# Order of stores, row transfers and loads in the first half of a Strassen MLP (DiT block, one core)

## Chip, cores and metric

One core of one Trainium2 chip runs the whole program. The metric is the time of one execution on the device in microseconds; lower is better.

## The reference

A transformer block with adaptive modulation (two sequences of 2048 tokens, 576 features, 16 heads), all in float32. The part that matters here is the MLP that ends it:

```python
xn2 = _ln(x, 1e-06)
xn2 = xn2 * (1 + sc_mlp[:, None, :]) + sh_mlp[:, None, :]
h = jax.nn.gelu(xn2 @ w1 + b1, approximate=False)     # 576 -> 2304
m = h @ w2 + b2                                       # 2304 -> 576
x = x + g_mlp[:, None, :] * m
```

## The kernel before

The kernel does modulation, attention and the output projection for one batch entry after the other, and then the MLP for all 4096 tokens. Both MLP products are computed by a seven-product (Strassen-Winograd) scheme, and the MLP is split into two halves by a round trip through DRAM.

**First half.** The tokens form NB = 8 blocks of 512, and the hidden features form HF = 9 pairs of column groups. A *job* is one block with one group: block n = job // 9, f = job % 9, so there are 72 jobs. A loop takes two jobs at a time, an even one and an odd one. In each job:

- PE runs `whole_part` (14 matmuls over the full 128-row chunks; the product number 1 goes to the bank `one`, written last) and `last_part` (8 matmuls for the last 64 features). Two sets of banks, one for even and one for odd jobs, hold the results.
- `hidden_made` empties the banks: ACT copies product 1 into a buffer `cs`, DVE combines the other six with it (four instructions), ACT applies Gelu (two), POOL makes the four sums that are the operands of the second half. There are three buffers `cs`, used in turn, so the copy of job j overwrites what job j - 3 left.
- `hidden_stored(job)` is a transfer, issued by SP, of one `cs` (896 KB) to the tensor `operands` in DRAM. It has to be done before the copy of three jobs later.

Beside this, `ahead(job)` prepares the rows of the next blocks, four tiles of 128 tokens (i = 0 to 3) per block, in four steps that lie two or three jobs apart: "load" fetches rows (SP), "turn" normalizes them (DVE statistics, an ACT square root, DVE) and writes them turned in 32 x 32 squares to DRAM (four SP transfers), "read" fetches them by feature (three SP transfers), "modulate" applies scale and shift (six ACT instructions and one of POOL). A generator says which step of which tile falls to which job; with a block that begins on an even job, nearly all fall to the even jobs, with the others to the odd ones. When a block begins, `token_sums` (four DVE instructions) makes the sums that its products need; for a block that begins on an odd job they are placed inside the even job before it.

SP, POOL, ACT and DVE run in the order of the program text (PE too), so in each pair of jobs the order on SP is: `ahead(job)`, `hidden_stored(job-2)`, `ahead(job+1)`, `hidden_stored(job-1)`, and then what the weights need. A transfer that waits on SP holds up all behind it.

In the same loop DVE makes the seven combinations of w2, two steps per pair of jobs (`weights_made`, in five chunks c = 0 to 3 and the tail): SP loads pieces into `w_first`, DVE adds and subtracts, SP stores the results with `stored` to the tensor `w_kept` in DRAM, 31 transfers of one 144-column piece for all seven products. At the end SP loads three of the combined weights (products 1, 2 and 6) back into `w_first` (`firsts_loaded`).

**Second half.** 56 products: for each block seven, in the order 1, 2, 6, 5, 7, 4, 3. Each needs one operand (1152 KB, `operand_loaded`), kept in three buffers in turn, and one combined weight (2232 KB, `weights_loaded`, seven in all). `sums_made(i)` makes the sums of an operand, on POOL for even and on DVE for odd products; `multiplied` is PE's part, some 7.8 us; `combined_blocks` and `finished` are DVE's, with the residual rows `xr` that SP loads for four of the seven products.

Where the buffers lie: operand 0 is in its own memory. When the last block's jobs have used a column of the first weight `wb`, its memory is free; there lie operand 1 and the weights of products 5, 7 and 4. Operand 2, the weight of product 3 and the sums of odd products lie in a new pool `hs`, which is opened after the first half. In the loop's last jobs SP loads operand 1 (after jobs 64 and 65, `at_job == 2`), weight 5 (after 66 and 67) and weight 7 (after 68 and 69); at the start of the second half it loads operand 2, then two gate rows, and in the loop of the products operand i + 3 once product i has been multiplied, and weights 4 and 3 after products 1 and 2.

Of the kernel before, what the change touches and what calls it, by code (L numbers as in the profile page):

```python
# [8 lines left out]
F32 = mybir.dt.float32  # L9
# [7 lines left out]
P = 128  # L17
# [5 lines left out]
FULL = 4  # L23
# [8 lines left out]
def dit_block(  # L32
# [724 lines left out]
    def block_of_small():  # L757
# [1275 lines left out]
        def ahead(job):  # L2033


            n, f = divmod(job, HF)

            def at(**offsets):
                for i in range(TPB):
                    for what, offset in offsets.items():  # L2040
                        m, g = divmod(job - 2 * i - offset, HF)
                        if g == 0 and m + 1 < NB and (m, i) > (0, 0):
                            yield what, (m + 1, i)

            for what, todo in at(turn=-2, read=0, modulate=2, load=-5):
                m, i = todo
                block, cols = xnts[m % 2], slice(i * P, (i + 1) * P)
                if what == "load":
                    rows_ahead[todo] = mlp_loaded(*todo, nc.sync)
                elif what == "turn":  # L2050
                    rows_ahead[todo] = tile_turned(rows_ahead[todo], nc.sync)
                elif what == "read":
                    turned_loaded(block, cols, rows_ahead.pop(todo), nc.sync)
                else:
                    turned_modulated(block, cols, 2, m // NBLK)
# [4 lines left out]
        def weights_made(c):  # L2060

            tail = c == 2 * FULL
            depth = 1 if tail else 2
            all_ = w_first[:, 0, 0 : 7 * depth * HALF].rearrange("p (i k f) -> p i k f", i=7, k=depth)
            more = w_first[:, 1, 0 : 28 * QUARTER].rearrange("p (i j f) -> p i j f", i=7, j=4)
            side = w_first[:, 2, 0 : depth * HALF].rearrange("p (k f) -> p k f", k=depth)
            rows = w2.rearrange("(k p) f -> p k f", p=P)
            tt = nc.vector.tensor_tensor

            def load():  # L2070
                for dst, k, n in ((all_[:, 0], 0, 0), (side, 0, 1), (all_[:, 1], 1, 0), (all_[:, 2], 1, 1)):
                    k0 = k * HF + c
                    nc.sync.dma_start(
                        out=dst, in_=rows[:, k0 : k0 + (depth - 1) * FULL + 1 : FULL, n * HALF : (n + 1) * HALF]
                    )

            def stored(j, src):
                nc.sync.dma_start(
                    out=w_kept[:, :, j * QUARTER : (j + 1) * QUARTER].rearrange("i p f -> p i f"), in_=src
                )  # L2080

            left, right = slice(0, QUARTER), slice(QUARTER, HALF)
            y11, y12 = all_[:, :, 0, left], all_[:, :, 0, right]
            steps = [
                load,
                lambda: None,
                lambda: tt(all_[:, 4], side, all_[:, 0], ALU.subtract),
                lambda: tt(all_[:, 6], all_[:, 2], side, ALU.subtract),
                lambda: tt(all_[:, 5], all_[:, 2], all_[:, 4], ALU.subtract),
                lambda: tt(all_[:, 3], all_[:, 5], all_[:, 1], ALU.subtract),  # L2090
            ]
            if tail:
                return [
                    *steps,
                    lambda: (
                        tt(more[:, :, 0], y12, y11, ALU.subtract),
                        [stored(28 + j, src) for j, src in enumerate((y11, y12, more[:, :, 0]))],
                    ),
                    *[lambda: None] * 3,
                ]  # L2100
            y21, y22 = all_[:, :, 1, left], all_[:, :, 1, right]
            return [
                *steps,
                lambda: (
                    tt(more[:, :, 1], y12, y11, ALU.subtract),
                    [stored(FULL * j + c, src) for j, src in enumerate((y11, y21, y22))],
                ),
                lambda: tt(more[:, :, 3], y22, y12, ALU.subtract),
                lambda: tt(more[:, :, 2], y22, more[:, :, 1], ALU.subtract),
                lambda: (  # L2110
                    tt(more[:, :, 0], more[:, :, 2], y21, ALU.subtract),
                    [stored(FULL * (3 + j) + c, more[:, :, j]) for j in range(4)],
                ),
                *[lambda: None] * 3,
            ]
# [4 lines left out]
        def firsts_loaded():  # L2120
# [1 line left out]
                weights_loaded(m, w_first[:, i, :])  # L2122

        spots = wb.rearrange("p f m k c -> p (f m k c)")
        operand.append(spots[:, 0 : HF * PAIR].rearrange("p (f c) -> p f c", f=HF))
        weight_spots = {
            m: spots[:, HF * PAIR + i * WSIZE : HF * PAIR + (i + 1) * WSIZE] for i, m in enumerate((5, 7, 4))
        }
        sums = {0: [first_sums[:, j] for j in range(3)]}

        def operand_parts(i):
# [21 lines left out]

        making_weights = [do for c in (0, 1, 2, 3, 2 * FULL) for do in weights_made(c)] + [firsts_loaded]

        rows_ahead = {}
        for i in (1, 2):
            nc.vector.memset(xs["tiles"][0][0:1, 0:1], 0.0)
            rows_ahead[1, i] = mlp_loaded(1, i, nc.gpsimd)
# [1 line left out]
        with tc.manual_schedule(  # L2161
            engines={mybir.EngineType.SP, mybir.EngineType.Pool, mybir.EngineType.Activation}
        ):
            for job in range(0, NB * HF, 2):
                (n0, f0), (n1, f1) = divmod(job, HF), divmod(job + 1, HF)
                ahead(job)
                hidden_stored(job - 2)
                whole_part(n0, f0, 0)
                if f1 == 0:
                    token_sums(n1)  # L2170
                last_part(n0, f0, 0)
                ahead(job + 1)
                hidden_stored(job - 1)
                hidden_made(n0, f0, 0)
                whole_part(n1, f1, 1)
                last_part(n1, f1, 1)
                if f1 == HF - 1 and n1 + 1 < NB:
                    token_sums(n1 + 1)
                hidden_made(n1, f1, 1)
                for _ in range(2):  # L2180
                    if job >= 2 and making_weights:
                        making_weights.pop(0)()
                if job == 2 * HF:
                    operand_loaded(0)
                if job == 4 * HF:
                    sums_made(0, slice(0, 3))
                at_job = job + 1 - (NB - 1) * HF
                if at_job == 2:
                    operand_loaded(1)
                for i, m in enumerate((5, 7)):  # L2190
                    if at_job == (4, 6)[i]:
                        weights_loaded(m, weight_spots[m])
        for job in (NB * HF - 2, NB * HF - 1):
            hidden_stored(job)
        stack.close()
# [4 lines left out]
        hs, close_hs = opened("hs")  # L2200
        rows_in_order = tc.manual_schedule(engines={mybir.EngineType.SP})
        rows_in_order.__enter__()
        operand.append(hs.tile([P, HF, PAIR], F32, name="operand2"))
        operand_loaded(2)
        weight_spots[3] = hs.tile([P, WSIZE], F32, name="w_last")
        ws = {m: w_first[:, i, :] for i, m in enumerate((1, 2, 6))} | weight_spots
        sums[0].append(hs.tile([P, FULL, P], F32, name="fourth"))
        sums_made(0, slice(3, 4))
        sums_odd = hs.tile([P, 4, FULL, P], F32, name="sums")
        sums[1] = [sums_odd[:, j] for j in range(4)]  # L2210
        ws = {m: w.rearrange("p (j f) -> p j f", f=QUARTER) for m, w in ws.items()}

        def stationaries(i):
# [4 lines left out]
        def multiplied(i):  # L2218
# [6 lines left out]
            for group in ((1,), (2, 6), (5, 7), *last):  # L2225
                ps = bank()[:, 0 : 2 * QUARTER].rearrange("p (a f) -> p a f", a=2)
                outs[group] = ps
                for a, m in enumerate(group):
                    out_m[m] = ps[:, a, :]
                    ends = m == group[-1]  # L2230
                    for c in range(FULL):
                        nc.tensor.matmul(  # L2232
                            out_m[m],
                            stationary[m][:, c, :],
                            w[:, FULL * (m - 1) + c, :],
                            start=a == 0 and c == 0,
                            stop=ends and c == FULL - 1 and m not in tails,
                        )
                    if m in tails:
                        t, j = tails[m]  # L2240
                        nc.tensor.matmul(  # L2241
                            out_m[m], x_[:, 2 * FULL, t * P : (t + 1) * P], w[:, j, :], start=False, stop=ends
                        )
# [59 lines left out]
        for i, (n, m) in enumerate(products):  # L2303
# [9 lines left out]
            xr = residual_rows(n, *quadrant, gate_bias) if quadrant else None  # L2313
            out_m, outs = multiplied(i)
            operand_loaded(i + 3)
            if i in (1, 2):
                weights_loaded((4, 3)[i - 1], weight_spots[(4, 3)[i - 1]])
            if i + 1 == len(products):
                last_finished(z12, out_m, outs, n, *quadrant, xr, gate)
                break  # L2320
# [68 lines left out]
```

## Time and profile before

| | us |
|---|---|
| median of three runs (3114.15 to 3115.0) | 3114.4 |
| the profiled execution, its own time | 3114.03 |
| its span, first to last instruction | 3111.4 |
| PE busy | 3059.0 (98%) |
| DVE busy | 1661.6 (53%) |
| ACT busy | 1491.8 (48%) |
| POOL busy | 954.1 (31%) |

The granted TensorE clock is 0.998 of full speed over the span. In the profile a row of a timeline gives the start (us from the span's first instruction), the duration, the engine, the line of the kernel, what is written from what, and a count of like instructions in a row; in brackets stands how long the engine had been idle before it, and what ended that. "SPq" is SP issuing a transfer. In the table by stretches the columns are the length, the busy time of PE, PE's weight load, DVE, ACT and POOL (with counts), the granted clock, the busy share of the DMA engines and what they moved in GB/s. A line of the chain of waits gives start, duration and what the end was waiting for.

### The profile page before, as it was taken

The page shows a single profiled execution, that of the slowest core. Times are in us where ns is not written, and L with a number is a line of the kernel's source. Part 1 is how long each engine was busy: PE and PEld are TensorE (multiplying, and loading weights), DVE is VectorE, ACT ScalarE, POOL GpSimd, SP SyncE. Part 2 cuts the span into 40 slices and gives each one's busy share as a digit, 9 for nine tenths or more (in the row PEclk, how much of TensorE's full clock was granted, in tenths as well). Part 3 has the DMA queues.
Part 4 walks back from the last instruction along what each step waited for, and adds up shares of the span by engine and source line. Part 5 has one row for each costly group of instructions (what it writes and reads, how often), then busy time and mean ns, then how long its engine had stood idle before and what let it go on. Part 6 is the DMA issues. An engine that isn't in the chain of part 4 may idle for free.

```text
span 3111.4 us, 51193 instructions
## 1 busy us (share of the span) xinstructions
PE 3059.0 (98%) x19079; PEld 1909.4 (61%) x19079; DVE 1661.6 (53%) x2525; ACT 1491.8 (48%) x2909; POOL 954.1 (31%) x1191
## 2 busy tenths in 40 slices
PE   8999999999999999999999999999999899999999
PEld 6884333333333788533333333368888788999999
DVE  6773444444443566444434444446666554676666
ACT  2336666766667023566666666633555543000000
POOL 4650100132231355200011210013444444555554
PEclk9999999999999999999999999999999999999999
DMA  5773332233332554311122322155877778755554
GB/s 150 188 145 86 102 93 58 66 94 98 93 100 68 193 128 79 85 47 34 47 57 73 86 66 59 57 146 168 247 225 224 216 215 295 289 192 194 205 191 158
DMA packets 443832, 413.52 MB, mean 133 GB/s; under 512 B 231512, under 2 KB 375896, under 8 KB 435448
## 3 DMA queue, kind: packets, MB, share of 16 engines
q1 hardware_dynamic: 398176, 310.84, 33.8%
q0 software_dynamic: 35968, 94.02, 11.2%
q10 hardware_dynamic: 9432, 5.31, 0.7%
q8 instruction: 153, 2.51, 0.3%
q14 instruction: 103, 0.84, 0.1%
HBM read 244.81 MB, written 154.75 MB: 128 GB/s over the span
## 4 chain that ended last, share of the span: by engine, by line
PE 85%; DMA 4%; DVE 4%; ACT 3%; SPq 2%; issue 1%; POOL 1%; DVEq 0%; ACTq 0%; POOLq 0%
PE b L1549 29%; PE b L1536 20%; PE b L2232 12%; PE s L1143 6%; PE s L1229 5%; PE m L1983 4%; PE s L411 4%; DMA operands<-cs 3%; PE b L2241 2%; SPq L1047 1%; PE s L1145 1%; PE m L1997 1%; PE s L1235 1%; PE one L1983 1%; ACT xnt L1064 1%
## 5 line engine op out<-in xcount | busy, mean ns | idle before, releaser
L1540 ACT ACTIVATE pt<-b 128x512 f32<-128x512 f32 x2048 | 1057.4, 608 | 481.4 <-PE b L1549 267.6
L1549 PE MATMUL b<-pt,vt 128*64 128x512 f32 x4096 | 935.0, 598 | 1.8 <-ACT pt L1540 1.8
L1549 PEld LDWEIGHTS b<-pt,vt 128*64 128x64 f32 x4096 | 271.8, 136 | 583.9 <-issue 437.7
L1536 PE MATMUL b<-qm,km 32*128 32x512 f32 x4096 | 563.9, 613 | 0.1
L1601 DVE TENSOR_TENSOR ot<-b,ot 128x512 f32<-128x512 f32 x192 | 132.7, 691 | 586.9 <-PE b L1549 586.9
L1536 PE MATMUL b<-qe,ke 16*128 16x512 f32 x2048 | 420.6, 791 | 0.0
L1536 PEld LDWEIGHTS b<-qm,km 32*128 32x128 f32 x4096 | 191.0, 184 | 271.0 <-ACT pt L1540 211.1
L1983 PE MATMUL m<-xnt,wb 128*128 128x256 f32 x864 | 213.2, 383 | 17.9 <-DVE cs L2017 17.0
L1143 PE MATMUL s<-wq,xnt 128*128 128x288 f32 x864 | 226.7, 406 | 2.0 <-ACT xnt L400 2.0
L1568 DVE RECIPROCAL den<-den 128x512 f32<-128x512 f32 x64 | 213.5, 3337 | 11.0 <-DMA den<-den_dram 11.0
L2249 ACT COPY one<-b 128x144 f32<-128x144 f32 x55 | 15.4, 279 | 410.2 <-PE b L2232 395.1
L1983 PE MATMUL m<-s,wb 128*128 128x256 f32 x864 | 210.0, 379 | 0.0
L1599 DVE COPY ot<-b 128x512 f32<-128x512 f32 x64 | 44.3, 691 | 273.0 <-PE b L1549 273.0
L1983 PEld LDWEIGHTS m<-xnt,wb 128*128 128x128 f32 x864 | 159.5, 191 | 41.4 <-DVE cs L2017 20.9
L1143 PEld LDWEIGHTS s<-wq,xnt 128*128 128x128 f32 x864 | 157.8, 190 | 37.5 <-ACT xnt L400 2.7
L1983 PEld LDWEIGHTS m<-s,wb 128*128 128x128 f32 x864 | 164.2, 190 | 22.3
L1536 PEld LDWEIGHTS b<-qe,ke 16*128 16x128 f32 x2048 | 107.1, 184 | 113.6 <-issue 112.8
L2021 ACT ACTIVATE cs<-cs,b_sb 128x512 f32<-128x512 f32 x144 | 100.5, 721 | 131.5 <-DVE cs L2016 131.4
L1064 ACT ACTIVATE xnt<-xnt,mod 128x128 f32<-128x128 f32 x244 | 99.9, 481 | 116.7 <-DMA weight_sums<-sums_kept 50.8
L1658 POOL DMA_DIRECT2D spare<-in_x_dram x32 | 17.8, 555 | 443.0 <-DVE met L796 443.0
L2023 POOL TENSOR_TENSOR cs<-cs 128x256 f32<-128x256 f32 x72 | 59.5, 826 | 294.1 <-ACT cs L2021 294.1
L2010 DVE TENSOR_TENSOR cs<-m,cs 128x512 f32<-128x512 f32 x72 | 48.8, 678 | 158.7 <-ACT cs L2009 111.1
(322 smaller groups left out, 4479.3 us busy)
## 6 DMA issues: line engine op xcount, KB each, us to landing
operands<-cs SPq DMA_DIRECT2D x72, 896.0 KB
operand<-operands SPq DMA_DIRECT2D x37, 1152.0 KB
wb<-operands SPq DMA_DIRECT2D x19, 1152.0 KB
spare<-in_x_dram POOLq DMA_DIRECT2D x64, 288.0 KB, 3.2
x_dram<-spare POOLq DMA_DIRECT2D x64, 288.0 KB, 2.5
qm<-qk SPq DMA_DIRECT2D x256, 64.0 KB
den<-den_dram SPq DMA_DIRECT2D x128, 128.0 KB
w_kept<-w_first SPq DMA_DIRECT2D x31, 504.0 KB
```

What stands on the lines that cost most here:

```text
L411: nc.tensor.matmul(outs[a], stationary(k, a), moving(k, a), start=(first and k == 0), stop=(not first and k == FULL - 1),)
L1064: nc.scalar.activation(part, part, AF.Identity, **affine(which, k, b))
L1143: nc.tensor.matmul(out_a, full[:, k, :], wq[:, k, f], start=k == 0, stop=False)
L1229: nc.tensor.matmul(out[m], x_[:, k, :], w_(k), start=k == 0, stop=k == 1 and m == 6)
L1536: nc.tensor.matmul(ps, k[r, keys], q[r, :], start=first, stop=not first)
L1540: nc.scalar.activation(pt[:, h, :], banks[2 * c + h], AF.Exp, scale=SCALE)
L1549: nc.tensor.matmul(acc[64 * h : 64 * h + 64, :], vt[:, v0 : v0 + 64], pt[:, h, :], start=pt is pts[0][0], stop=pt is pts[-1][0],)
L1568: nc.vector.reciprocal(den, den)
L1601: nc.vector.tensor_tensor(ot, acc, ot, ALU.add)
L1983: nc.tensor.matmul(out_m[m], wb[:, f, slot[m], k, :], moving[m](k), start=k == 0 and m in (1, 2, 5, 6), stop=k == 1 and m == 1,)
L2021: nc.scalar.activation(part, part, AF.Gelu, bias=b1_sb[:, g : g + 1])
L2232: nc.tensor.matmul(out_m[m], stationary[m][:, c, :], w[:, FULL * (m - 1) + c, :], start=a == 0 and c == 0, stop=ends and c == FULL - 1 and ...
```

## The change

1. `ahead` goes through the steps in the order read, turn, load, modulate, and within each over the tiles; before, it went through the tiles, and within each through turn, read, modulate, load. In a job in which a tile is turned and another modulated, the square root now comes first on ACT.
2. `hidden_stored(job - 2)` comes before `ahead(job)`, and `hidden_stored(job - 1)` before `ahead(job + 1)`.
3. The tensor `w_kept` is laid out by chunk, so the pieces of one chunk lie side by side: a full chunk is stored in three transfers (1, 2 and 4 columns wide) instead of seven, the tail in two instead of three. They are put on a list and issued at the start of the next pair of jobs, behind `hidden_stored(job - 2)`. PE's index into the weight follows.
4. Operand 2 lies in the memory of `wb` beside operand 1, and both are loaded after jobs 66 and 67; weight 5 is loaded after jobs 68 and 69. The sums of odd products lie in `wb` too. Weights 4 and 3 lie in `hs`. Weights 7, 4 and 3 are loaded after products 0, 1 and 2.

```diff
-                for i in range(TPB):
-                    for what, offset in offsets.items():
+                for what, offset in offsets.items():
+                    for i in range(TPB):
...
-            for what, todo in at(turn=-2, read=0, modulate=2, load=-5):
+            for what, todo in at(read=0, turn=-2, load=-5, modulate=2):
...
-            def stored(j, src):
-                nc.sync.dma_start(
-                    out=w_kept[:, :, j * QUARTER : (j + 1) * QUARTER].rearrange("i p f -> p i f"), in_=src
-                )
+            def stored(j, count, src):
+                j += 7 * c if not tail else 28
+                dst = w_kept[:, :, j * QUARTER : (j + count) * QUARTER].rearrange("i p f -> p i f")
+                to_store.append(lambda: nc.sync.dma_start(out=dst, in_=src))
...
-                        [stored(28 + j, src) for j, src in enumerate((y11, y12, more[:, :, 0]))],
+                        stored(0, 2, all_[:, :, 0, :]),
+                        stored(2, 1, more[:, :, 0]),
...
-                    [stored(FULL * j + c, src) for j, src in enumerate((y11, y21, y22))],
+                    stored(0, 1, y11),
+                    stored(1, 2, all_[:, :, 1, :]),
...
-                    [stored(FULL * (3 + j) + c, more[:, :, j]) for j in range(4)],
+                    stored(3, 4, more.rearrange("p i j f -> p i (j f)")),
...
-        operand.append(spots[:, 0 : HF * PAIR].rearrange("p (f c) -> p f c", f=HF))
+        OSIZE = HF * PAIR
+        operand += [spots[:, i * OSIZE : (i + 1) * OSIZE].rearrange("p (f c) -> p f c", f=HF) for i in range(2)]
         weight_spots = {
-            m: spots[:, HF * PAIR + i * WSIZE : HF * PAIR + (i + 1) * WSIZE] for i, m in enumerate((5, 7, 4))
+            m: spots[:, 2 * OSIZE + i * WSIZE : 2 * OSIZE + (i + 1) * WSIZE] for i, m in enumerate((5, 7))
         }
+        odd_sums = spots[:, 2 * OSIZE + 2 * WSIZE :][:, 0 : 4 * FULL * P].rearrange(
+            "p (j k c) -> p j k c", j=4, k=FULL
+        )
...
                 (n0, f0), (n1, f1) = divmod(job, HF), divmod(job + 1, HF)
+                hidden_stored(job - 2)
+                while to_store:
+                    to_store.pop(0)()
                 ahead(job)
-                hidden_stored(job - 2)
...
                 last_part(n0, f0, 0)
+                hidden_stored(job - 1)
                 ahead(job + 1)
-                hidden_stored(job - 1)
...
-                if at_job == 2:
+                if at_job == 4:
                     operand_loaded(1)
-                for i, m in enumerate((5, 7)):
-                    if at_job == (4, 6)[i]:
-                        weights_loaded(m, weight_spots[m])
+                    operand_loaded(2)
+                if at_job == 6:
+                    weights_loaded(5, weight_spots[5])
...
-        operand.append(hs.tile([P, HF, PAIR], F32, name="operand2"))
-        operand_loaded(2)
-        weight_spots[3] = hs.tile([P, WSIZE], F32, name="w_last")
+        for m in (4, 3):
+            weight_spots[m] = hs.tile([P, WSIZE], F32, name=f"w{m}")
...
-                            w[:, FULL * (m - 1) + c, :],
+                            w[:, 7 * c + m - 1, :],
...
-            if i in (1, 2):
-                weights_loaded((4, 3)[i - 1], weight_spots[(4, 3)[i - 1]])
+            if i < 3:
+                weights_loaded((7, 4, 3)[i], weight_spots[(7, 4, 3)[i]])
```

5 lines of the change are left out of this document (2 added, 3 removed).

## The prediction

> **What bounds the kernel now.** I read the page's parts 1 and 4 first, then the order of PE in time, then who waited for whom, then SP's queue.
>
> ```profile
> span 3111.4 us, 51193 instructions
> PE 3059.0 (98%) x19079; PEld 1909.4 (61%) x19079; DVE 1661.6 (53%) x2525; ACT 1491.8 (48%) x2909; POOL 954.1 (31%) x1191
> 2122.76:2660.83 538.07, 513.42 (x2593) 454.66 (x2593) 307.45 (x519) 260.68 (x457) 238.87 (x318) 0.99 0.77 233
> ```
>
> The third line is the table by stretches for the first MLP half: 538 us, DMA engines 77% busy. PE is the bound, so a change pays only where PE stands still. PE's timeline gives that:
>
> ```profile
> 2122.76 1.96 PE L1983 MATMUL m<-xnt,wb 128*128 128x256 f32 x8 [0.90 <-issue]
> 2194.69 1.99 PE L1983 MATMUL m<-xnt,wb 128*128 128x256 f32 x8 [1.46 <-DVE cs L2017]
> 2343.57 1.99 PE L1983 MATMUL m<-xnt,wb 128*128 128x256 f32 x8 [0.74 <-DVE cs L2017]
> 2467.78 1.99 PE L1983 MATMUL m<-xnt,wb 128*128 128x256 f32 x8 [1.13 <-DVE cs L2017]
> 2579.12 2.00 PE L1983 MATMUL m<-xnt,wb 128*128 128x256 f32 x8 [0.35 <-DVE cs L2017]
> 2628.22 1.89 PE L1983 MATMUL m<-xnt,wb 128*128 128x256 f32 x8
> 2636.35 2.07 PE L1983 MATMUL one<-xnt,wb 128*128 128x256 f32 x4 [2.78 <-ACT cs L2009]
> 2660.83 2.12 PE L2232 MATMUL b<-w_first,operand 128*128 128x144 f32 x16
> ```
>
> Except for 2636.35 (inside job 68) these are starts of jobs 0, 10, 30, 46, 61, 68 and of the first product, "job 72". An undisturbed job takes 7.00 us (61 to 68: 49.10 / 7), so 72 want 504.0 and got 538.07: 34.07 us are lost. Start minus first start minus 7 x number gives the lag: 1.93 at job 10, 10.81 at 30, 23.02 at 46, 29.36 at 61, 29.46 at 68, 34.07 at the end. So 1.93 is lost before job 10, then 8.88, 12.21 and 6.34 in three clusters, 0.10, and 4.61 in job 68. The clusters lie in blocks 2, 4 and 6 and run into the next one: nine jobs a block, so these blocks begin on an even job, and their row work falls into the even jobs.
>
> ```profile
> ACT cs L2009 <- DMA operands<-cs: 70.3, 17, 11.0
> DVE cs L2010 <- ACT cs L2009: 111.1, 32, 12.2
> PE m L1983 <- DVE cs L2017: 17.0, 18, 1.6
> ```
>
> From the waits (us, times, longest): ACT's copy into a cs buffer waits until the store of three jobs ago has left it, DVE waits for ACT, PE for DVE. Why the store is late shows the timeline of all engines in job 20 (last row: the copy of job 21):
>
> ```profile
> 2266.96 0.73 POOL L2026 TENSOR_TENSOR cs<-cs 128x256 f32<-128x256 f32 x1
> 2270.88 1.64 ACT L1064 ACTIVATE xnt<-xnt,mod 128x128 f32<-128x128 f32 x4
> 2272.32 0.21 DVE L279 BATCH_NORM_AGGREGATE mv<-st 128x2 f32<-128x12 f32 x1
> 2273.31 1.28 ACT L281 ACT_TABLE_LOAD   x1
> 2274.80 0.35 ACT L2009 COPY cs<-one 128x256 f32<-128x256 f32 x1
> 2276.55 1.98 SPq L1047 DMA_DIRECT2D turned<-squares  x4
> 2278.64 1.09 SPq L2031 DMA_DIRECT2D operands<-cs  x2
> 2282.97 0.37 ACT L2009 COPY cs<-one 128x256 f32<-128x256 f32 x1 [1.92 <-DMA operands<-cs]
> ```
>
> POOL finished job 18's sums at 2267.69. SP issued their store at 2278.64, 10.95 us later, having sat in order behind the four row transfers, which waited for DVE. It landed at 2282.9, when PE had long wanted the buffer (job 21 ends near 2279.8).
>
> **The change, part by part.** *Stores ahead of row transfers* (SP). With hidden_stored(job-2) first, job 18's store goes at 2267.7 and lands by 2272 to 2276 (4.3 us as above, or 8.8 behind a burst):
>
> ```profile
> 2218.66 8.81 DMA operands<-cs
> 2266.01 9.75 DMA xnt<-turned
> L2078 SPq DMA_DIRECT2D w_kept<-w_first x31: 359/852/3530, 2194.7 to 2590.3; - x31
> ```
>
> That is 3 to 7 us before job 21 wants it, so the clusters should go: 8.88 + 12.21 + 6.34 = 27.43, less two block starts of 1.4 (block starts, below), 24.6. Not all: I keep 1.6 for bursts of weight stores, an estimate (one stall of the size above). Gain 23.0, between 12 and 24.6. What now stands behind the store's wait for POOL on SP are the row transfers, three reads, four turns and a load per row job. A read lands in 9.75 us (second row, from the chain) and is wanted two jobs, 14 us, later: 4.25 us to spare. That hides it.
>
> *Roots ahead of modulations* (ACT). In the same rows ACT modulated from 2270.88 to the table load at 2273.31 (2.4 us), and then took the root. Turned round, it loads the table (1.28 us) and takes the root when mv is ready at 2272.5; the modulations end near 2275.1, where the copy of job 20 began at 2274.80. So the copy is 0.3 late, up to 1.6 where mv is later, and the squares about 2 us earlier. PE wants the copied bank only a job later: 0, bounds +1 and -2 over the half.
>
> *Weight stores in three pieces.* 31 issues become 14 (4 x 3 + 2): 17 x 0.85 us of SP time, which waits anyway; the bytes stay. They go one pair of jobs later, and their next load comes 1.5 pairs after that. Cost 0; the burst behind the 8.81 above (1.0 us of the second cluster's 8.88) now comes behind the even store.
>
> *Block starts.*
>
> ```profile
> 2184.95 1.08 DVE L1953 TENSOR_TENSOR s<-xnt 128x512 f32<-128x512 f32 x1 [0.87 <-ACT xnt L1064]
> 2190.17 0.29 ACT L281 ACTIVATE std<-mv,eps 128x1 f32<-128x1 f32 x1 [3.18 <-DVE mv L279]
> ```
>
> At odd blocks DVE does the token sums and a row's norm before it empties job 8's banks; PE then waits 1.46 (row 2194.69), and likewise two more times, some 4.5 in all. The diff leaves this order. With copies on time the sums may start some tenths earlier: 0.7 gained in all, an estimate, bounds 0 and 4.5.
>
> *Loads at the end of the half.*
>
> ```profile
> 2607.44 2.51 SPq L2118 DMA_DIRECT2D w_first<-w_kept  x3
> 2609.99 0.68 SPq L2152 DMA_DIRECT2D wb<-operands  x1
> 2613.90 0.37 SPq L2031 DMA_DIRECT2D operands<-cs  x1
> 2635.92 0.37 ACT L2009 COPY cs<-one 128x256 f32<-128x256 f32 x1 [11.03 <-DMA operands<-cs]
> wb<-operands SPq DMA_DIRECT2D x19, 1152.0 KB
> wb<-w_kept SPq DMA_DIRECT2D x3, 2232.0 KB
> 2610.00:2620.00 10.00, 10.00 (x51) 8.91 (x51) 2.62 (x5) 2.65 (x5) 4.77 (x7) 1.00 1.03 411
> ```
>
> Job 64's store stood behind three weights (6.86 MB) and operand 1 (1.18 MB), and job 68 lost 4.61. Operand 1 now comes behind that store: at 411 GB/s it lands 2.9 us sooner, the copy at 2633.0, which is PE's own time for that bank; DVE's emptying still makes job 69 about 1.5 late. Gain 3.1, bounds 0 and 4.6. [...] After that, operands 1 and 2 (2.36 MB) take the place of weight 5 (2.29), weight 5 that of weight 7, one block column of wb sooner: equal bytes, 0.
>
> *Start of the second half.*
>
> ```profile
> 2674.01 8.99 DMA xr<-x_dram
> 2681.71 3.21 PE L2232 MATMUL b<-w_first,first_sums 128*128 128x144 f32 x24 [2.42 <-POOL first_sums L2146]
> 2686.00 4.71 DVE L2146 TENSOR_TENSOR sums<-sums,operand 128x512 f32<-128x512 f32 x1
> 2690.76 3.21 PE L2232 MATMUL b<-wb,sums 128*128 128x144 f32 x24 [0.94 <-DVE sums L2146]
> 2696.50 2.12 PE L2232 MATMUL b<-wb 128*128 128x144 f32 x16
> 2704.34 2.12 PE L2232 MATMUL b<-wb,operand 128*128 128x144 f32 x16
> ```
>
> A product takes 7.84 (last two rows); four took 35.67, so 4.31 were lost, first to operand 2 (POOL's sums), then to xr, behind which DVE makes the sums of product 3. Operand 2 is now there; but weight 7 (5.6 us at 411) is queued ahead of xr. Counting from product 0's start, xr landed at 22.2; without operand 2 (2.9) and with weight 7 it lands near 24 to 25. POOL's bias (1.4), DVE's add and two sums (0.7 to 0.8 each) follow in 3.7 if POOL does not slow them: ready at 28.2, wanted at 23.5 + 2.2 = 25.7 (three products and the first row's 2.12 us). Loss 2.5, gain 1.8, bounds +4.3 and -2.8. From product 4 on nothing changes.
>
> **Sum.** 23.0 + 0 + 0 + 0.7 + 3.1 + 1.8 = 28.6. The profiled execution took 3114.03 (2.6 around its span), 0.4 under the median 3114.4: 3085.4 against it, 3086 as a median. Nothing else can be had: 34.07 + 4.31 = 38.4 is all of PE's loss here, which gives 3076.
>
> **Rivals.**
> *Weight 7 takes over.* DVE's second sum stretches to 4.71 beside POOL, as in the row above, and xr is late: the sums are ready at 31.8 instead of 28.2, product 3 loses 6.1, and PE another 1 in coming up again, a loss of 7.1 for my 2.5, so 3114.4 - 24 = 3090. For it: SP's one queue; against: POOL's next sums wait for operand 4, queued later still. [...]
> *The DMA engines become the bound.* Bursts already fill them (1.03 above). If early stores still land late, half of the 24.6 stays: 12.3 + 0.7 + 3.1 + 1.8 = 17.9, so 3096.5. Against: the 8.81 landing would still be in time.
> *It does not do what it says.* The stores were late from DMA alone: 3113. Against: the 10.95 us on SP.
> *Slower: rows come late.* Reads now stand behind a wait for POOL and weight stores that can take 3.53 us to issue. From 4.25 us of delay on, ACT waits in order at the modulation with the cs copies behind it, 27 times (four a block, seven blocks, one done before). Each microsecond past it costs up to 27; past 5.3 it eats the 28.6. At 5.7 us: 3114.4 - 28.6 + 39 = 3125. Against: no ACT wait for a read appears in the waits of before.
>
> **Numbers.** Forecast 0.62, weight 7 0.13, DMA 0.17: all faster, 0.92. No effect 0.04, rows late 0.04. About 0.2%, 6 us, is what a measurement tells apart. Likeliest 3086, its own range 3079 to 3092; the 8-in-10 range reaches from all of the loss gone, 3076, to past the DMA rival, 3100.
>
> **What would show it.** Right: SP's operand store straight after POOL's last sum, ahead of the four turns; the ACT wait for operands<-cs down from 70 us to under 20; blocks 2, 4, 6 at 7.00 us a job; a first half of 506 to 512 us. Wrong: ACT waiting on xnt<-turned, or DMA at 1.0 while the copies still wait; a loss past 6 us before product 4. The forecast fails if PE's stalls only move to another wait in the same jobs.

## The result, and the profile after

The changed kernel takes 3090.7 us (median of four runs, 3090.14 to 3092.17) against 3114.7 for the kernel before in the same session (its three runs above and one of 3119.28): a ratio of 0.992 with the 95% interval [0.9903, 0.9938]. It is faster by 24.0 us where 28.6 were forecast.

The first two lines of the page of the changed kernel, and then its table by stretches (columns as before) for the first MLP half and for the first eight products of the second:

```profile
span 3089.8 us, 51183 instructions
PE 3055.7 (99%) x19079; PEld 1910.9 (62%) x19079; DVE 1666.5 (54%) x2525; ACT 1492.6 (48%) x2909; POOL 956.3 (31%) x1191
```
```profile
2124.64:2632.32 507.68, 505.25 (x2592) 451.83 (x2593) 310.98 (x519) 261.63 (x457) 241.61 (x318) 1.00 0.80 244
2632.32:2705.64 73.32, 66.59 (x514) 66.16 (x513) 50.99 (x73) 3.50 (x10) 34.80 (x28) 0.95 0.71 270
```

The first half shrank from 538.07 to 507.68 us. Where PE still stands shows its timeline in order; these are the first job, all stops of the first half that a wait explains, and products 0, 3, 4, 7 and 8 (of products 3 and 7 the row after the wait):

```profile
2124.64 1.96 PE L1983 MATMUL m<-xnt,wb 128*128 128x256 f32 x8 [0.90 <-issue]
2195.70 2.00 PE L1983 MATMUL m<-xnt,wb 128*128 128x256 f32 x8 [0.83 <-DVE cs L2017]
2322.45 1.99 PE L1983 MATMUL m<-xnt,wb 128*128 128x256 f32 x8 [0.48 <-DVE cs L2017]
2449.20 1.99 PE L1983 MATMUL m<-xnt,wb 128*128 128x256 f32 x8 [0.49 <-DVE cs L2017]
2611.22 2.00 PE L1983 MATMUL m<-xnt,wb 128*128 128x256 f32 x8 [0.62 <-DVE cs L2017]
2632.32 2.12 PE L2238 MATMUL b<-w_first,operand 128*128 128x144 f32 x16
2660.57 4.88 PE L2238 MATMUL b<-wb 128*128 128x144 f32 x24 [2.36 <-DVE wb L2152]
2667.98 2.12 PE L2238 MATMUL b<-wb 128*128 128x144 f32 x16
2698.23 4.88 PE L2238 MATMUL b<-w_first,wb 128*128 128x144 f32 x24 [4.36 <-DVE wb L2152]
2705.64 2.12 PE L2238 MATMUL b<-w_first,wb 128*128 128x144 f32 x16
```

The three clusters are gone; what is left are block starts (2195.70, 2322.45, 2449.20) and one stop near the end (2611.22). The half lost 507.68 - 504.0 = 3.68 us, before 34.07. The second half got worse: product 4 starts 35.66 after product 0, a loss of 4.30 (before 4.31), and product 8 starts 73.32 after it where eight products take 62.72, a loss of 10.60. Before, nothing was lost from product 4 to 8.

The waits of the changed kernel from 2100 us on (total, times, longest), the rows that answer to those of before and the new one:

```profile
DVE cs L2010 <- ACT cs L2009: 33.7, 23, 9.3
...
ACT cs L2009 <- DMA operands<-cs: 12.8, 3, 8.1
...
PE b L2238 <- DVE wb L2152: 6.7, 2, 4.4
...
PE m L1983 <- DVE cs L2017: 2.4, 4, 0.8
```

ACT's wait for stores fell from 70.3 to 12.8, PE's for DVE in the first half from 17.0 to 2.4. The same place as in job 20 before, from the timeline of all engines of the changed kernel:

```profile
2265.98 0.73 POOL L2026 TENSOR_TENSOR cs<-cs 128x256 f32<-128x256 f32 x1
2266.73 0.37 SPq L2031 DMA_DIRECT2D operands<-cs  x1
...
2271.07 0.29 ACT L281 ACTIVATE std<-mv,eps 128x1 f32<-128x1 f32 x1 [0.28 <-DVE mv L279]
2271.28 1.63 ACT L1064 ACTIVATE xnt<-xnt,mod 128x128 f32<-128x128 f32 x4
```

POOL's last sum ends at 2266.71 and SP issues the store 0.02 us later (before: 10.95); the root stands ahead of the modulations.

The profiled executions took 3114.03 and 3091.24 us, 22.79 less: 30.39 less in the first half, 6.30 more from product 0 to PE's last matmul (443.51 to 449.81), 1.88 more before job 0, and 0.58 less elsewhere. The 1.88 isn't the change's: the code up to there is the same, and job 0 started between 2122.8 and 2125.4 in the profiles of this study.

### The profile page after: what moved, and what is told of

Its sections match the earlier page's. It is cut to its first block, busy times and chain, and to the rows that moved or that the text cites. A ratio compares the mean times of both kernels' runs of the same rounds, so it can differ in the third digit from the quotient of the medians.

```text
span 3089.8 us, 51183 instructions
## 1 busy us (share of the span) xinstructions
PE 3055.7 (99%) x19079; PEld 1910.9 (62%) x19079; DVE 1666.5 (54%) x2525; ACT 1492.6 (48%) x2909; POOL 956.3 (31%) x1191
## 4 chain that ended last, share of the span: by engine, by line
PE 95%; DVE 2%; DMA 1%; ACT 1%; issue 1%; POOL 0%; DVEq 0%; ACTq 0%; POOLq 0%; SPq 0%
PE b L1549 30%; PE b L1536 20%; PE b L2238 11%; PE m L1983 11%; PE s L1143 7%; PE s L1229 5%; PE s L411 4%; PE m L1997 2%; PE one L1983 2%; PE b L2247 2%; PE s L1145 1%; DMA operands<-cs 1%; PE s L1235 1%; PE s L422 1%; DMA xr<-x_dram 0%
```

## The experiments

Below, "lag" is a job's start minus job 0's start minus 7 us a job. At job 63 it holds what the first half lost before its final loads.

Two theories stood against each other. *Order on SP*: the stores' place in SP's queue is the cause, so part 2 does nearly all and the rest nothing. *Margin*: PE stops only when a copy's delay exceeds what the second set of banks covers; each part takes some delay away, so the effects overlap. A third, *DMA load*, put the gain down to the fewer, longer weight stores.

### One part at a time

**Stores first, alone** (before with part 2).

```diff
-                ahead(job)
                 hidden_stored(job - 2)
+                ahead(job)
...
-                ahead(job + 1)
                 hidden_stored(job - 1)
+                ahead(job + 1)
```


> The kernel before with one edit: each operand store stands ahead of the row transfers of its job. Measured is the lag of the first half (start of the first product less start of the first job less 504.0: 34.07 before, 3.68 after) and the loss of the second half's start (nine product starts, less eight times 7.84: 4.31 before, 10.60 after). Theory 'order on SP': the late stores are all of the three clusters, so the lag falls to 7 to 10 (the 3.6 that job 68 had more before stay, about 1 for a burst of weight stores), the start loss stays at 4.3, time 3087 to 3091. Rival 'DMA load' (fewer and wider weight stores made the stores land in time): the lag stays above 20, time above 3100.

Measured: 3093.47 us, ratio 0.9932 [0.9915, 0.9949]; lag 6.38 at job 63 (before 29.46), 11.27 at product 0. Part 2 alone brings 20.3 us, as *order on SP* asked, though less than forecast (a lag of 7 to 10 at product 0, 3087 to 3091 us). *DMA load*, with a lag above 20, is excluded as the sole cause: here the weight stores are as before. The largest single stop is that of job 68, in PE's timeline:

```profile
2615.22 1.13 PE L1983 MATMUL one<-xnt,wb 128*128 128x256 f32 x4 [2.80 <-ACT cs L2009]
```

**Row transfers first again** (the changed kernel without part 2).

```diff
-                hidden_stored(job - 2)
-                while to_store:
-                    to_store.pop(0)()
                 ahead(job)
+                hidden_stored(job - 2)
+                while to_store:
+                    to_store.pop(0)()
...
-                hidden_stored(job - 1)
                 ahead(job + 1)
+                hidden_stored(job - 1)
```


> The kernel after with one part undone: the row transfers stand ahead of the operand stores again; order of steps, weight stores and loads stay changed. Theory 'order on SP': the clusters in blocks 2, 4 and 6 come back, lag 20 to 30, time 3107 to 3117. Rival 'DMA load': lag under 10, time under 3097. Rival 'roots first': part of it stays away, lag 10 to 18.

Measured: 3096.82 us, 0.9942 [0.9926, 0.9959]; lag 8.77 at job 63, 9.93 at product 0. That fells *order on SP* as the sole cause, which wanted 20 to 30: with the stores behind the row transfers, parts 1 and 3 still take 20.7 of the 29.5 away. The figures lie just where *DMA load* put them (under 10, under 3097), so this run alone would speak for it; the run before this one excludes it as the sole cause. The store of job 18 is still issued 9.20 us after POOL's last sum (2267.07 to 2276.27).

What then keeps PE going? Job 22 shows it. In this kernel, from the timelines of PE, ACT and DVE, these are PE's product 1 of job 22, the root on ACT, the copy, DVE's last instruction on the banks of job 22, and the start of job 24, which writes to them again:

```profile
2284.59 1.03 PE L1983 MATMUL one<-xnt,wb 128*128 128x256 f32 x4
...
2286.64 0.29 ACT L281 ACTIVATE std<-mv,eps 128x1 f32<-128x1 f32 x1 [0.86 <-DVE mv L279]
...
2289.15 0.35 ACT L2009 COPY cs<-one 128x256 f32<-128x256 f32 x1
...
2291.57 0.69 DVE L2017 TENSOR_TENSOR cs<-cs,m 128x512 f32<-128x512 f32 x1
...
2293.41 1.89 PE L1983 MATMUL m<-xnt,wb 128*128 128x256 f32 x8
```

In the kernel before, the same from the root on:

```profile
2290.42 0.29 ACT L281 ACTIVATE std<-mv,eps 128x1 f32<-128x1 f32 x1
2290.62 0.35 ACT L2009 COPY cs<-one 128x256 f32<-128x256 f32 x1
...
2294.19 0.69 DVE L2017 TENSOR_TENSOR cs<-cs,m 128x512 f32<-128x512 f32 x1
...
2294.93 1.99 PE L1983 MATMUL m<-xnt,wb 128*128 128x256 f32 x8 [0.99 <-DVE cs L2017]
```

Here the copy began 3.5 us after PE's last write of product 1 (2285.62 to 2289.15), and DVE was done 1.15 us before PE wanted the banks. The margin for this copy is thus some 4.7 us, if DVE is free. In the kernel before it was not: the root came only just ahead of the copy, DVE waited for it, finished that row, and began on the banks 1.29 us after the copy had ended (2290.97 to 2292.26). PE stopped for 0.99, though this copy waited for no store.

Product 1 has a limit of its own. In the kernel before, the copy of job 23, and PE's row right behind it, product 1 of job 24:

```profile
2301.23 0.37 ACT L2009 COPY cs<-one 128x256 f32<-128x256 f32 x1 [5.59 <-DMA operands<-cs]
```
```profile
2301.65 1.13 PE L1983 MATMUL one<-xnt,wb 128*128 128x256 f32 x4 [1.27 <-ACT cs L2009]
```

PE waited here for the copy of the job just before, of the other set; the same holds of all five such stops in the kernel before. So the two sets of banks do not separate the jobs at product 1. In the kernel before, between jobs 11 and 67, PE's waits behind copies that themselves waited for a store add up to 8.4 us, and those at even jobs, behind a root on ACT and the row that DVE finished first, to some 12 us (2.3 of it at the block starts of jobs 28 and 46).

**Old step order** (the changed kernel without part 1), and **step order alone** (before with part 1).

```diff
-                for what, offset in offsets.items():
-                    for i in range(TPB):
+                for i in range(TPB):
+                    for what, offset in offsets.items():
...
-            for what, todo in at(read=0, turn=-2, load=-5, modulate=2):
+            for what, todo in at(turn=-2, read=0, modulate=2, load=-5):
```
The second makes these lines the other way round, in the kernel before.

> The kernel after with one part undone: the steps of ahead in the old order (modulations ahead of the root). Lag at the start of job 63 (before the loads at the end of the half): 29.46 before, 2.65 after, 6.38 with the stores first alone, 8.77 with all but the stores first. Theory 'margin': several delays add up in an even job and PE stands still only for what is over a margin, so any two of the three parts nearly do: lag at job 63 of 2.6 to 5. Rival 'roots': the order of the steps is what the stores alone lacked: 5.5 to 6.5.

> The kernel before with one edit: steps of ahead in the order read, turn, load, modulate (the root ahead of the modulations, the squares some 2 us sooner on SP). Theory 'margin': lag at job 63 of 12 to 25. Rival 'roots carry it': 8 to 11. That neither moves it (above 27 in both) would say that only the two together do.

Measured, one run each: without it 3090.88 us, lag 2.63 (with it 2.65); alone 3108.56, lag 21.07. Alone it removes 8.4 us of lag, on top of the rest nothing. The size of the 8.4 is rough: the kernel before ran once on that chip, in 3110.68 us, without a profile, and the 29.46 is from an execution of 3114.03 on another; by the times it is 2.1. Earlier roots bring the squares earlier to SP, and while the store waits behind these, it comes earlier too: job 18's store left 9.22 us after POOL's sum in place of 10.95.

**Weight stores as before** (the changed kernel without part 3), and **weight pieces alone** (before with part 3).

```diff
-            def stored(j, count, src):
-                j += 7 * c if not tail else 28
-                dst = w_kept[:, :, j * QUARTER : (j + count) * QUARTER].rearrange("i p f -> p i f")
-                to_store.append(lambda: nc.sync.dma_start(out=dst, in_=src))
+            def stored(j, src):
+                nc.sync.dma_start(
+                    out=w_kept[:, :, j * QUARTER : (j + 1) * QUARTER].rearrange("i p f -> p i f"), in_=src
+                )
```
The second is the reverse, in the kernel before.

> The kernel after with one part undone: weight stores of one column each, 31, issued where DVE makes them. Theory 'margin': lag at job 63 of 2.6 to 5. Rival 'pieces': the weight stores are what the stores first alone lacked: 5.5 to 6.5, with stalls behind the bursts near jobs 14, 29 and 40 as there.

> The kernel before with one edit: weight stores in three pieces, a pair of jobs later, behind the even operand store; row transfers stay ahead of it, steps and loads as before. Theory 'margin': part of the clusters goes, lag at job 63 of 12 to 25. Rival 'pieces carry it' (the 8.77 left without stores first is their doing): 8 to 11.

Measured, one run each: without it 3092.3 us, lag 4.69; alone 3101.67, lag 16.49. The part costed at nothing removes 13.0 us of lag by itself (9.0 by the times, against the same 3110.68). The weight stores in the changed kernel, as SP issues them (count, then least, median and most ns):

```profile
L2080 SPq DMA_DIRECT2D w_kept<-w_first x14: 360/467/1437, 2199.8 to 2565.4; - x14
```

Before it was 31 issues with a median of 852 ns, ahead of the next row transfers and stores. Whether the issue time, the longer pieces or the later place does it was not separated.

Together, the lag at job 63 (us) under all eight combinations; some have part 4, which acts only after job 64 (without it the changed kernel has the same 2.65, below):

| | rows first | stores first |
|---|---|---|
| neither part 1 nor 3 | 29.46 (before) | 6.38 |
| part 1 | 21.07 | 4.69 |
| part 3 | 16.49 | 2.63 |
| parts 1 and 3 | 8.77 | 2.65 (after) |

Alone the parts remove 23.1, 8.4 and 13.0, together 44.5; all at once remove 26.8. That is what *margin* asks for, and the four runs of parts 1 and 3 lie in the ranges that it gave. It doesn't hang on the rough sizes: with the rows first, parts 1 and 3 take 20.7 us of lag away, with the stores first 3.7. *DMA load* as the sole cause falls by the same table: with the weight stores as before, stores first leave 6.38.

### The loads

**Loads as before** (the changed kernel without part 4).

```diff
-                if at_job == 4:
+                if at_job == 2:
                     operand_loaded(1)
-                    operand_loaded(2)
-                if at_job == 6:
-                    weights_loaded(5, weight_spots[5])
+                for i, m in enumerate((5, 7)):
+                    if at_job == (4, 6)[i]:
+                        weights_loaded(m, weight_spots[m])
...
-            if i < 3:
-                weights_loaded((7, 4, 3)[i], weight_spots[(7, 4, 3)[i]])
+            if i in (1, 2):
+                weights_loaded((4, 3)[i - 1], weight_spots[(4, 3)[i - 1]])
```
(with the memory of operand 2 and of the sums as before)

> The kernel after with one part undone: operand 2, weights 7, 5, 4 and the sums of odd products lie and are loaded where they were before. Theory 'weight 7 in the queue': the start loss falls back from 10.6 to 3 to 5, job 68 loses 3 to 4.6 again (it lost 0.9), lag 6 to 8, time 3086 to 3089. Rival 'the start came 28 us earlier and is limited by itself' (operand 3 and 6 are late however the weights are queued): the start loss stays at 8 to 11, time 3093 to 3095.

Measured: 3088.13 us, 0.9923 [0.9907, 0.994]; lag 2.65 at job 63 and 6.43 at product 0, second-half loss 4.47 (from product 0 to the last matmul, beyond 56 products of 7.84). Time, lag and start loss (4.30) lie where *weight 7 in the queue* put them. Its stops at job 68 and at products 2 and 3 are those of before:

```profile
2611.32 1.13 PE L1983 MATMUL one<-xnt,wb 128*128 128x256 f32 x4 [2.64 <-ACT cs L2009]
...
2656.00 3.21 PE L2236 MATMUL b<-w_first,first_sums 128*128 128x144 f32 x24 [2.39 <-POOL first_sums L2148]
...
2665.04 3.21 PE L2236 MATMUL b<-wb,sums 128*128 128x144 f32 x24 [0.93 <-DVE sums L2148]
```

So by the profiles part 4 gains 2.75 in the first half (6.43 to 3.68) and loses 6.30 in the second (4.47 to 10.77): a net loss of 3.55. The two ratios have overlapping intervals, so the times alone do not show it.

**Weight 7 between the last two stores** (the changed kernel, its load moved from behind product 0).

```diff
-        for job in (NB * HF - 2, NB * HF - 1):
-            hidden_stored(job)
+        hidden_stored(NB * HF - 2)
+        weights_loaded(7, weight_spots[7])
+        hidden_stored(NB * HF - 1)
...
-            if i < 3:
-                weights_loaded((7, 4, 3)[i], weight_spots[(7, 4, 3)[i]])
+            if i in (1, 2):
+                weights_loaded((4, 3)[i - 1], weight_spots[(4, 3)[i - 1]])
```


> The kernel after, but weight 7 is loaded between the stores of the last two jobs, a stretch in which the DMA engines are 14% busy, instead of after operand 3. Theory 'weight 7 in the queue': the rows xr land 5 to 6 us sooner and operand 6 in time, start loss 0 to 3, time 3081 to 3084. Rival 'limited by itself': DVE's sums still wait and stretch beside POOL, start loss 7 to 10, time 3088 to 3091.

Measured: 3086.04 us, 0.991 [0.9893, 0.9926]. Its profiled execution took 3080.88, the other three 3085.8 to 3086.8, so its trace doesn't show what those lost, and the median misses the 3081 to 3084 of the theory. In the trace the rows xr land 19.3 us after product 0's start, 5.2 sooner than in the changed kernel, as the theory had it. The second half loses 1.64, at product 3 only, and shows a new thing:

```profile
2652.99 4.73 DVE L2152 TENSOR_TENSOR wb<-wb,operand 128x512 f32<-128x512 f32 x1
2653.41 2.54 POOL L2152 TENSOR_TENSOR first_sums<-wb 128x512 f32<-128x512 f32 x2
2655.91 1.25 POOL L2152 TENSOR_TENSOR first_sums<-first_sums,wb 128x512 f32<-128x512 f32 x1
2657.78 3.21 PE L2239 MATMUL b<-wb 128*128 128x144 f32 x24 [1.21 <-DVE wb L2152]
```

DVE's second sum for product 3 takes 4.73 us beside three of POOL's, in place of 0.69. The rows xr now come early enough for DVE's sums to fall into POOL's.

**Rows xr early too** (the one above, with the first xr loaded ahead of operand 3).

```diff
-        def residual_rows(n, t, a, bias):
+        def residual_loaded(n, t, a):
             xr = hs.tile([P, 2, HALF], F32, name="xr", bufs=4)
             nc.sync.dma_start(out=xr, in_=rows_of(n, t, a, x1_dram))
+            return xr
...
-            xr = residual_rows(n, *quadrant, gate_bias) if quadrant else None
+            if i == 0:
+                early = residual_loaded(n, 0, 0)
+            xr = residual_rows(n, *quadrant, gate_bias, early if i == 1 else None) if quadrant else None
```


> The kernel with weight 7 between the last two stores, and now the first residual rows xr are loaded right after the gate rows, ahead of operand 3. With weight 7 early alone PE still waited 1.21 us at product 3, because DVE's second sum took 4.73 us beside POOL's sums of operand 4 (0.69 alone). Theory 'contention': rows that land some 3 us sooner let DVE make its sums before operand 4 is there, both sums take 0.7, the start loss falls from 1.64 to under 0.6. Rival 'operand 3 is the limit': its landing holds DVE's sums, the loss stays at 1.2 to 2. Time either way 3081 to 3086.

Measured: 3086.46 us, 0.9907 [0.9892, 0.9922]. Product 3 loses nothing now, as *contention* said, but product 7 does; the second half loses 7.05, and the time is no better than above. Whether the three runs without a trace above stopped at product 7 too isn't shown. DVE's second sum of product 3, then DVE's and POOL's sums and PE at product 7:

```profile
2652.71 0.69 DVE L2152 TENSOR_TENSOR wb<-wb,operand 128x512 f32<-128x512 f32 x1
...
2684.84 9.17 DVE L2152 TENSOR_TENSOR wb<-wb 128x512 f32<-128x512 f32 x4
...
2685.97 2.50 POOL L2152 TENSOR_TENSOR first_sums<-wb 128x512 f32<-128x512 f32 x2
...
2692.86 6.01 PE L2239 MATMUL b<-w_first,wb 128*128 128x144 f32 x24 [3.82 <-DVE wb L2152]
```

**Weight 6 later** (the one above, with weight 6 loaded after jobs 66 and 67, ahead of operand 1).

```diff
-            for i, m in enumerate((1, 2, 6)):
+            for i, m in enumerate((1, 2)):
...
                 if at_job == 4:
+                    weights_loaded(6, w_first[:, 2, :])
                     operand_loaded(1)
```


> As the one with early rows, and weight 6 (2232 KB) is loaded after jobs 66 and 67 instead of together with weights 1 and 2 after 64 and 65. Theory 'ring order': job 64's store has 2.3 MB less ahead of it and lands some 5.6 us sooner, the 1.0 that jobs 68 and 69 still lose goes (lag 3.7 to 2.7), 1 us less in time. Rival 'only moved': the store of job 66, now behind weight 6 and two operands, comes late for job 69's copy, and the lag stays at 3.5 or grows to 6.

Measured: 3085.48 us, 0.9903 [0.9888, 0.9918]. The lag stays at 2.66 from job 63 to product 0: with one weight less queued ahead of job 64's store, the last stop of the half is gone, as the first theory said. The second half still loses 6.26.

**The changed kernel again**, on the chip of these two, so that they can be compared.

> The kernel after itself, for the comparison on the same chip: 3090 to 3092, start loss 10 to 11; both variants above are then 5 to 10 us faster if the waits shown are what they cost.

Measured: 3091.34 us, 0.9922 [0.9908, 0.9935]; second-half loss 11.20. The two variants are 4.9 and 5.9 us faster, the low end of what was expected.

**Weight 3 later** (weight 6 later, with weight 3 loaded after product 3, behind operand 6).

```diff
-            if i in (1, 2):
-                weights_loaded((4, 3)[i - 1], weight_spots[(4, 3)[i - 1]])
+            if i in (1, 3):
+                weights_loaded((4, 3)[i // 2], weight_spots[(4, 3)[i // 2]])
```


> As the one with weight 6 later, and weight 3 is loaded behind operand 6 (after product 3) instead of ahead of it (after product 2). With early rows PE still lost about 6 at product 7: operand 6 landed late behind weights 4 and 3, POOL's sums of it held up the next rows xr, DVE came late to the sums of product 7 and made them beside POOL's of product 8 (9.17 us for four, 2.6 alone). Theory 'weights ahead of operands': operand 6 lands 5.6 us sooner, the wait at product 7 goes, second-half loss under 1.5, time 3079 to 3082. Rival 'order of POOL and DVE alone': the two engines still meet at products 7 and 8, loss 5 to 7, time 3085 to 3087.

Measured: 3078.6 us (3077.86 to 3082.49), 0.9888 [0.9871, 0.9904]: faster than both kernels, its interval clear of the changed kernel's 0.9922 [0.9908, 0.9935], though it just touches that of its first measurement, [0.9903, 0.9938], and overlaps that of weight 6 later. The runs were on different chips, where the kernel before took 3114.07 and 3114.82. The time is a little under the 3079 to 3082 expected. In its timeline SP issues operand 6 ahead of weight 3, and the sums of product 7 no longer take 9 us:

```profile
2661.44 0.32 SPq L2158 DMA_DIRECT2D operand<-operands  x1
2661.82 0.42 SPq L2120 DMA_DIRECT2D w<-w_kept  x1
...
2681.07 3.71 DVE L2152 TENSOR_TENSOR wb<-wb 128x512 f32<-128x512 f32 x4
```

The second half loses 0.16. PE's only stops by a wait in both halves are the three block starts (2.65 in all). Between this kernel and *weight 6 later* only weight 3's place differs, and in the profiles the loss falls from 6.26 to 0.16: the stop at product 7 came from the order of the loads. DVE's and POOL's sums still meet there, but for 3.71 us only.

## Why the prediction was right or wrong

The forecast, 3086 us, missed by 4.7, and the measured time lay within its range; the sign and the main mechanism held. That the range was met is in part luck: the three gains of the first half came out 3.3 us larger than forecast, the start of the second half 8.1 worse. With the gains as forecast the time would have been about 3094, outside 3079 to 3092. By its terms:

- **Clusters, 23.0: too small.** I kept 1.6 for bursts; nothing stayed. The lag at job 61 is 2.65, all of it block starts, so the whole 24.6 came. The signs named for it appeared: the store straight behind POOL's sum, the wait at 12.8, the half at 507.68. But the reading of job 20 was too simple. The copy of job 21 at 2282.97 stopped no matmul: PE asked for it only at product 1 of job 22, at 2284.97. After it PE stopped from job 24 on. Of the stops between jobs 11 and 67 more (some 12 us) ended with DVE finishing a row behind a late root than with a copy that itself waited for a store (8.4). Apart from the block starts both kinds are gone there in the changed kernel; with the stores first alone one stop behind a store stays (0.62) and two behind such a row (0.82 and 1.45).
- **Roots, 0, and weight stores, 0: right beside the rest, wrong as statements on these parts.** Alone they remove 8.4 and 13.0 us of lag (2.1 and 9.0 by the times). Costing them with the stores already first made them look empty; "PE wants the copied bank only a job later" left out that DVE waits for the root before it empties the banks.
- **Block starts, 0.7: gained 1.9** (4.5 to 2.65). The waits at jobs 10, 28 and 46 are 0.83, 0.48 and 0.49 now and were 1.46, 1.12 and 1.13. The diff leaves DVE's order there. The early stores do most of it: with the stores first alone the waits are 0.83, 0.48 and 0.44, with the rows first again 0.97, 1.13 and 1.12. That copies on time let DVE come earlier is what I take as the way it works.
- **Job 68, 3.1: 3.6.** Its loss fell from 4.61 to 1.03. The copy's wait for job 64's store fell from 11.0 to 8.1, by the 2.9 forecast; what stayed is due to the weights ahead of that store: taking weight 6 from there removed it (3.68 us lost by product 0, then 2.66).
- **Start of the second half, +1.8: it was -6.3.** This is the step that failed, by 8.1 us. Up to product 3 the working was close. From SP's, POOL's and DVE's timelines of the changed kernel:

```profile
2642.72 0.77 SPq L2158 DMA_DIRECT2D operand<-operands  x1
2643.54 0.43 SPq L2120 DMA_DIRECT2D wb<-w_kept  x1
...
2645.48 0.37 SPq L2274 DMA_DIRECT2D xr<-x_dram  x1
...
2656.99 1.41 POOL L2275 TENSOR_TENSOR xr<-xr,gate 128x576 f32<-128x576 f32 x1 [11.47 <-DMA xr<-x_dram]
...
2659.82 0.69 DVE L2152 TENSOR_TENSOR wb<-wb,operand 128x512 f32<-128x512 f32 x1
...
2677.44 3.10 POOL L2152 TENSOR_TENSOR first_sums<-operand 128x512 f32<-128x512 f32 x2 [11.03 <-DMA operand<-operands]
...
2683.67 1.84 DVE L2283 TENSOR_TENSOR r<-r,xr 128x576 f32<-128x576 f32 x1 [2.52 <-POOL xr L2275]
...
2690.19 9.19 DVE L2152 TENSOR_TENSOR wb<-wb 128x512 f32<-128x512 f32 x4
...
2691.32 2.52 POOL L2152 TENSOR_TENSOR first_sums<-wb 128x512 f32<-128x512 f32 x2
```

The rows xr landed 24.6 after product 0's start (forecast 24 to 25), the sums were ready at 28.2 (28.2), and PE waited 2.36 (2.5). I left out what such a wait costs behind itself: the 24 matmuls after it took 4.88 us instead of 3.10, so the loss was 4.30. And "from product 4 on nothing changes" was false. Operand 6 stood behind weights 7, 4 and 3 and landed at 2677.3, POOL made its sums late and the rows xr after them, DVE waited for these, and so DVE's sums of product 7 ran beside POOL's of product 8: four took 9.19 instead of 2.62, a wait of 4.36 and slow matmuls again. The weight 3 experiment, which puts operand 6 ahead of one weight, removed this stop.

The terms as measured, 24.6 + 1.9 + 3.6 - 6.3, make 23.8, beside 24.0 between the medians. (Two slips in the working change little: the weight burst lies in the first cluster, not the second, and 4.71 in place of 0.69 would make the sums of the weight 7 rival ready at 32.2 rather than 31.8.) The rivals:

- **Weight 7 takes over (0.13)** gave 3090, the measured time, but with a loss at product 3 of 7.1, where 4.30 was measured and DVE's second sum took 0.69. That it is weight 7 that makes xr late was right, the place and size of the rest were not. Its 1 us for PE to come up again was an estimate; in the changed kernel the 24 matmuls after the wait took 4.88 us for 3.10, 1.78 more.
- **DMA bound (0.17), no effect, rows late:** none came. The first half's DMA engines were busier (0.80 for 0.77) and the stores in time, but for those at the final loads (two of ACT's three waits for a store, 10.9 of 12.8 us). In the waits from 2100 us on ACT waits at a modulation for a read once, for 1.0 us.

## What to carry to other kernels

Two sets of banks and three buffers hide a delay up to a margin (some 4.7 us for the copy of job 22 here), so measure the margin first (lag by job, and at one job the time to spare), look for every engine that stands between the buffer and the matmul, and then ask of each edit whether it brings the delay below it; the effects of single edits did not add up here (44.5 us of lag one by one, 26.8 together). When a load is moved later in a queue, follow every load behind it to its first user, not only the next one. And keep sums on DVE and on POOL out of each other's time: one that took DVE 0.69 us took 4.73 beside POOL's here.

## What the runs showed of the hardware

**DVE and POOL in each other's way.** A 128x512 sum on DVE took 0.69 us alone and 4.73 beside three of POOL's; four took 2.62 alone (at 2669.75 in the changed kernel) and 9.17 to 9.19 beside POOL's. In the 4.73 case, *weight 7 between the last two stores*, DVE's sum ran from 2652.99 to 2657.72, over all three of POOL's (2653.41 to 2657.16), of which the third took 1.25 us. It isn't DVE alone that loses: from 2660.43 on in the changed kernel DVE's sums took 1.79 us each and POOL's three 4.76 in place of 3.79.

**A short wait of PE costs more than itself, but not always.** After 2.36 us without work the next 24 matmuls took 4.88 us; after 2.39 us in the kernel with loads as before, 3.21. The clock of the first and what the DMA engines moved soon after, from the table by stretches of the changed kernel:

```profile
2660.57:2665.45 4.88, 4.88 (x26) 4.88 (x27) 4.64 (x6) 0.00 (x0) 4.80 (x4) 0.65 0.96 408
```
```profile
2665.00:2670.00 5.00, 5.00 (x43) 5.00 (x42) 4.53 (x11) 0.28 (x1) 1.33 (x2) 1.00 1.05 444
```

The granted clock was 0.65 there and back at 1.00 behind it. Over the fourteen profiles, from job 1 to the last product: of PE's 31 waits between 0.9 and 1.6 us none was followed by a lower clock, of the 13 between 2.1 and 2.7 us eight were, and of the 11 from 2.7 us up all. The clock was then 0.50 for 3.41 us, after two of these 11 for 6.83. In the kernels before and after, the waits with the lower clock behind them were those of 2.36, 2.74, 2.78 and 4.36 us, while one of 2.42 and eleven from 0.94 to 1.59 had none. What decides between 2.1 and 2.7 us, where waits fell on both sides, was not shown.

**DMA.** The engines moved 444 GB/s over the 5 us of the second row, where the prediction reckoned with 411.
